# Attention layer's weights and first input on GpSimd's queue, in the place of in_proj's weights; first stripe's edge stores on ScalarE's queue

## The chip, the cores and the metric

The kernel runs on one core of one Trainium2 chip. The metric is the time of one execution on the device in microseconds (us). Several executions are measured and their median is compared. Times inside an execution come from one profiled execution and count from the start of its span, which runs from its first to its last instruction.

The engines are PE (TensorE: matmuls; PEld is its loading of weights), DVE (VectorE), ACT (ScalarE), POOL (GpSimd) and SP (SyncE). Each takes its own instructions in order. Transfers (DMA) are issued by an engine's queue and carried by 16 DMA engines.

## The reference

Two layers, each with a group norm in front and a residual behind, on an image batch of 4 x 384 channels x 64 x 64:

```python
# layer 0: a state-space layer over the 4096 tokens of an image
x = x + _L0_conv_ref(_gn(x), ...)
# layer 1: attention of every pixel to the 7 x 7 pixels around it, 12 heads of 32 channels
x = x + _L1_conv_ref(_gn(x), ...)

def _L1_conv_ref(x, w_qkv, b_qkv, w_proj, b_proj, rel_bias):
    ...
    qkv = jnp.einsum('oc,bchw->bohw', w_qkv, x) + b_qkv[None, :, None, None]
    ...
    q, k, v = (qkv[:, 0] * scale, qkv[:, 1], qkv[:, 2])
    pad = ((0, 0), (0, 0), (0, 0), (p, p), (p, p))
    k_pad = jnp.pad(k, pad, mode='edge')
    v_pad = jnp.pad(v, pad, mode='edge')
    logits = jnp.stack([jnp.einsum('bnchw,bnchw->bnhw', q, k_pad[..., di:di + H, dj:dj + W]) for di in range(ws) for dj in range(ws)], axis=-1)
    logits = logits + rel_bias.reshape(nh, ws * ws)[None, :, None, None, :]
    attn = jax.nn.softmax(logits, axis=-1)
    ...
    out = jnp.einsum('oc,bchw->bohw', w_proj, out) + b_proj[None, :, None, None]
```

## The kernel before

**Two stages.** `layer0` goes through 4 images of 16 chunks of 256 tokens; each chunk passes the input projection (L409, weights `w_in`), a causal convolution, the scan over 16 states (L623 on DVE, L635 on POOL) and the output projection (L695, weights `w_out`). Its result goes to a DRAM tensor `x1` for each image (L710) and is read back by `layer1`. `layer1` goes through 4 images of 8 stripes of 8 pixel rows. A stripe is prepared by `projected`, a generator whose steps are worked in between the blocks of the stripe before; only the first stripe is prepared alone, before any block.

**The first stripe.** `projected` loads eleven rows of `x1` into `xr` (L860), normalises them on DVE into `xn` (L869), computes the keys (L882 on PE, copied by ACT at L887, with edges copied by POOL at L895 to L903), then the values, two pixel rows at a time (L915, copied to `v` by DVE at L922), and then the queries (L945, L950). Matmuls of the first stripe write to the four PSUM banks of the tag `lg`; `v` has three buffers, so the fourth copy waits until everything stored from the first is done.

**The values in DRAM.** Padded values go to a DRAM tensor `vd` of 70 x 70 pixels. Each pixel row is written by three stores: the 64 pixels (L932, 96 KB), three copies of the first pixel (L933) and three of the last (L937, 4.5 KB each). The top row of the image goes to four rows of `vd`. For the first stripe these are 14 rows and so 42 stores. `window` (L963) then reads, for each block of 8 x 16 pixels, the 14 x 22 pixels around it into `vw`, by 14 loads.

**Weights.** At the head of `layer1`, `bias`, `w_qkv` and `w_pj` are allocated in the pool `wt`, in this order, which starts where the first pool of `layer0`, `w0`, started with `w_in`. `w_in` takes 18,432 bytes of each partition, `bias` 14,784, `w_qkv` 13,824 and `w_pj` 4,608. The mask and position terms `bias` are loaded from a DRAM tensor `bm` that was built during `layer0` (L1092). Nine small matmuls (L841, PSUM tile `pvb`) turn the bias of the values into one of the output, added to `pjb` by DVE (L846); `pjb` is first read at the end of a stripe (L1067). The group statistics of the last image (`group_stats`, L229; PE, DVE and one ACT step, `grs`) are computed after the first stripe is prepared, ahead of the first block.

**Order.** In both layers PE, DVE, ACT and POOL work in the order of the program text (`manual_schedule`). SP's transfers are ordered by a planner, which may put a transfer ahead of others written before it; SP takes the planned order one by one, and a transfer whose waits are not met holds up those behind it. Every transfer from SP or ACT counts up one of eight completion counters, taken in turn in the planned order, and first waits until the previous transfer on that counter has landed. In the kernel before all transfers are issued by SP.

Of the kernel before, what the change touches and what calls it, by code (L numbers as in the profile page):

```python
# [8 lines left out]
F32 = mybir.dt.float32  # L9
AF = mybir.ActivationFunctionType  # L10
ALU = mybir.AluOpType
# [3 lines left out]
P = 128  # L15
C = 384
NJ = C // P
# [31 lines left out]
def two_layers(  # L49
# [21 lines left out]
    nc = tc.nc  # L71
# [97 lines left out]
    with nc.allow_non_contiguous_dma(reason="small vectors, one element per partition"):  # L169
# [5 lines left out]
        qkb = column(qkv_b, 3 * NJ, "qkb", const)  # L175
        pjb = column(proj_b, NJ, "pjb", const)
# [15 lines left out]
    with tc.tile_pool(name="ps_fold", bufs=1, space=PSUM) as fps:  # L192
        pb0 = fps.tile([P, 512], F32, name="pb0")
        for m in range(2 * ND):
            for j in range(NJ):
                nc.tensor.matmul(
                    pb0[:, m : m + 1], w_in[:, j, m * P : (m + 1) * P], lnb[:, j : j + 1],
                    start=(j == 0), stop=(j == NJ - 1),
# [622 lines left out]
    def layer1(x1s, mvs, gms):  # L821
        scale = HD**-0.5
        with ExitStack() as es:
            es.enter_context(tc.manual_schedule(engines=in_step))
            ps_l = es.enter_context(tc.tile_pool(name="ps_l", bufs=4, space=PSUM))
            ps_t = es.enter_context(tc.tile_pool(name="ps_t", bufs=2, space=PSUM))
            ps_v = es.enter_context(tc.tile_pool(name="ps_v", bufs=1, space=PSUM))
            ps = es.enter_context(tc.tile_pool(name="ps1_", bufs=1, space=PSUM))
            wt = es.enter_context(tc.tile_pool(name="wt", bufs=1))
            w2 = es.enter_context(tc.tile_pool(name="v2_", bufs=2))  # L830

            bias = wt.tile([P, NH, NK], F32, name="bias")
            w_qkv = wt.tile([P, NJ, 3 * C], F32, name="w_qkv")
            nc.sync.dma_start(w_qkv, qkv_wT.rearrange("(k p) m -> p k m", p=P))
            w_pj = wt.tile([P, NJ, C], F32, name="w_pj")
            nc.sync.dma_start(w_pj, proj_wT.rearrange("(k p) m -> p k m", p=P))

            pvb = ps_t.tile([P, 512], F32, tag="pt", name="pvb")
            for m in range(NJ):
                for j in range(NJ):  # L840
                    nc.tensor.matmul(  # L841
                        pvb[:, m : m + 1], w_pj[:, j, m * P : (m + 1) * P],
                        qkb[:, 2 * NJ + j : 2 * NJ + j + 1],
                        start=(j == 0), stop=(j == NJ - 1),
                    )
            nc.vector.tensor_tensor(pjb, pjb, pvb[:, :NJ], ALU.add)  # L846
            vds = [dram.tile([WP, WP, C], F32, tag="vd", name=f"vd_{b}") for b in range(NB)]

            def bank(pool, tag):
                return pool.tile([P, 512], F32, tag=tag, name=f"{tag}_ps")  # L850

            def projected(b, s, h, pool=ps, tag="mm"):


                gm, vd = gms[b], vds[b]
                lo, hi = RB * s, min(HW, RB * s + RB + PAD)
                n = hi - lo
                xr = w2.tile([P, NJ, RB + PAD, HW], F32, tag="xr", name=f"xr_{b}_{s}")
                xn = w2.tile([P, NJ, RB + PAD, HW], F32, tag="xn", name=f"xn1_{b}_{s}", bufs=1)
                nc.sync.dma_start(  # L860
                    xr[:, :, :n, :].rearrange("p k r c -> p k (r c)"),
                    x1s[b][:, lo * HW : hi * HW].rearrange("(k p) t -> p k t", p=P),
                )
                q = w2.tile([P, NJ, NBLK, RB, CB], F32, tag="q", name=f"q_{b}_{s}")
                k = w2.tile([P, NJ, RW, WP], F32, tag="k", name=f"k_{b}_{s}")
                h["q"], h["k"] = q, k
                yield
                for j in range(NJ):
                    nc.vector.tensor_scalar(  # L869
                        xn[:, j, :n, :], xr[:, j, :n, :], gm[:, j, 0:1], gm[:, j, 1:2],  # L870
                        ALU.subtract, ALU.mult,
                    )

                old = 0 if s == 0 else PAD
                if s:
                    nc.sync.dma_start(k[:, :, : RW - RB, :], h["before"][:, :, RB:, :])
                for m in range(NJ):
                    for r0, r1 in ((0, PAD), (PAD, n)) if s == 0 else ((PAD, n),):
                        cols = (r1 - r0) * HW
                        pk = bank(pool, tag)  # L880
                        for j in range(NJ):
                            nc.tensor.matmul(  # L882
                                pk[:, :cols], w_qkv[:, j, C + m * P : C + (m + 1) * P],
                                xn[:, j, r0:r1, :].rearrange("p r c -> p (r c)"),
                                start=(j == 0), stop=(j == NJ - 1),
                            )
                        act(  # L887
                            k[:, m, PAD + r0 : PAD + r1, PAD : PAD + HW],
                            pk[:, :cols].rearrange("p (r c) -> p r c", c=HW),
                            AF.Identity, bias=qkb[:, NJ + m : NJ + m + 1],  # L890
                        )
                    yield
                new = k[:, :, PAD + old : PAD + n, :]
                edge = [P, NJ, n - old, PAD]
                nc.gpsimd.tensor_copy(  # L895
                    new[:, :, :, 0:PAD], new[:, :, :, PAD : PAD + 1].broadcast_to(edge)
                )
                nc.gpsimd.tensor_copy(
                    new[:, :, :, PAD + HW :],
                    new[:, :, :, PAD + HW - 1 : PAD + HW].broadcast_to(edge),  # L900
                )
                if s == 0:
                    nc.gpsimd.tensor_copy(  # L903
                        k[:, :, :PAD, :], k[:, :, PAD : PAD + 1, :].broadcast_to([P, NJ, PAD, WP])
                    )
                if s == NXT - 1:
                    nc.gpsimd.tensor_copy(
                        k[:, :, PAD + n :, :],
                        k[:, :, PAD + n - 1 : PAD + n, :].broadcast_to([P, NJ, RW - PAD - n, WP]),
                    )  # L910
                for r0 in range(old, n, 2):
                    rows = min(2, n - r0)
                    pv = bank(pool, tag)
                    for j in range(NJ):
                        nc.tensor.matmul(  # L915
                            pv[: rows * HW, :C],
                            xn[:, j, r0 : r0 + rows, :].rearrange("p r c -> p (r c)"),
                            w_qkv[:, j, 2 * C :],
                            start=(j == 0), stop=(j == NJ - 1),
                        )  # L920
                    v = w2.tile([P, C], F32, tag="v", name=f"v_{b}_{s}_{r0}", bufs=3)
                    nc.vector.tensor_copy(v[: rows * HW, :], pv[: rows * HW, :C])  # L922
                    for r in range(rows):
                        img = lo + r0 + r
                        src = v[r * HW : (r + 1) * HW, :]
                        to = [img + PAD]
                        if img == 0:
                            to = list(range(PAD + 1))
                        if img == HW - 1:
                            to = list(range(PAD + img, WP))  # L930
                        for y in to:
                            nc.sync.dma_start(vd[y, PAD : PAD + HW, :], src)  # L932
                            nc.sync.dma_start(  # L933
                                vd[y, 0:PAD, :].unsqueeze(0),
                                src[0:1, :].unsqueeze(1).broadcast_to([1, PAD, C]),
                            )
                            nc.sync.dma_start(  # L937
                                vd[y, PAD + HW :, :].unsqueeze(0),
                                src[HW - 1 : HW, :].unsqueeze(1).broadcast_to([1, PAD, C]),
                            )  # L940
                    yield
                for m in range(NJ):
                    pq = bank(pool, tag)
                    for j in range(NJ):
                        nc.tensor.matmul(  # L945
                            pq, w_qkv[:, j, m * P : (m + 1) * P],
                            xn[:, j, :RB, :].rearrange("p r c -> p (r c)"),
                            start=(j == 0), stop=(j == NJ - 1),
                        )
                    nc.vector.tensor_scalar(  # L950
                        q[:, m, :, :, :].rearrange("p b r c -> p r b c"),
                        pq.rearrange("p (r b c) -> p r b c", r=RB, b=NBLK),
                        qkb[:, m : m + 1], scale, ALU.add, ALU.mult,
                    )
                    yield
# [131 lines left out]

            todo = [(b, s) for b in range(NB) for s in range(NXT)]
            stripes = [{} for _ in todo]
            ahead = projected(*todo[0], stripes[0], ps_l, "lg")  # L1090
            next(ahead)
            nc.sync.dma_start(bias.rearrange("p h k -> p (h k)"), bm)  # L1092
            for _ in ahead:
                pass
            vw = window(*todo[0], 0)
            for part in group_stats(mvs[NB - 1], gms[NB - 1], ps, f"b{NB - 1}"):
                part()

# [124 lines left out]
```

## Time and profile before

| what | us |
|---|---|
| median of 4 runs | 8267.8 |
| lowest and highest | 8261.52 and 8272.43 |
| the profiled execution | 8261.52 |
| its span | 8259.5 |
| last matmul of layer 0 (L695) ends, about | 5931.4 |
| first matmul on the first stripe (L882) | 5946.5 |
| first matmul of the first block (L978) | 5987.45 |
| PE busy in the span | 7510.5 |
| DVE, POOL, ACT busy in the span | 6988.1, 6985.4, 5892.2 |
| mean granted TensorE clock (1 is full speed) | 0.949 |

The span is cut by the profile into forty slices. In the first 28, layer 0, PE, DVE, POOL and ACT are all busy for some eight tenths or more; in the last twelve, layer 1, PE is busy for nine tenths or more and the others for less. The DMA engines are busy for one to three tenths in nearly every slice. The passage between the layers is a small part of one slice, so it is read from the chain of waits, the timeline and windows of a few microseconds.

### The profile page before, as it was taken

The numbers are of one execution on the slowest core, as the hardware profiler recorded it, in microseconds if no ns is written. First come the engines' busy times: TensorE is split into PE (matmuls) and PEld (weight loads), VectorE is DVE, ScalarE is ACT, GpSimd is POOL, SyncE is SP. The second block draws the span as 40 slices with busy tenths as digits, with TensorE's granted clock in tenths as the row PEclk, the third lists the DMA queues.
The fourth block names the chain that finished last, engine by engine and source line by source line (L and its number), as shares of the span: only waits on it lengthen the run. The fifth ranks groups of instructions, "written<-read, shape, count | busy, mean of one in ns | idle before, by whom it ended". The sixth has DMA issues, their size and how long they took to land. (4 is left out here: it accounts for less than half of the span.)

```text
span 8259.5 us, 144369 instructions
## 1 busy us (share of the span) xinstructions
PE 7510.5 (91%) x48570; PEld 5814.9 (70%) x48570; DVE 6988.1 (85%) x12725; ACT 5892.2 (71%) x15613; POOL 6985.4 (85%) x4247
## 2 busy tenths in 40 slices
PE   7998998899899889988998999899799999999999
PEld 6777777777777777777777777777555555555555
DVE  5999999999999999999999999999666666666666
ACT  5888888888888888888878888888455455454455
POOL 4999999999999999999999999999677777677777
PEclk9999999999999999999999999999899999999999
DMA  3212211221121112112211211121223233232322
GB/s 109 65 60 70 74 58 57 69 68 59 65 76 62 55 63 75 59 65 72 66 53 59 69 58 55 62 69 51 81 84 87 85 88 88 81 88 84 89 82 64
DMA packets 327528, 583.40 MB, mean 71 GB/s; under 512 B 62940, under 2 KB 211180, under 8 KB 326660
## 3 DMA queue, kind: packets, MB, share of 16 engines
q1 hardware_dynamic: 326788, 574.17, 22.3%
q8 instruction: 387, 6.34, 0.3%
q14 instruction: 353, 2.89, 0.1%
HBM read 471.49 MB, written 84.73 MB: 67 GB/s over the span
## 5 line engine op out<-in xcount | busy, mean ns | idle before, releaser
L635 POOL TENSOR_TENSOR hs<-hs,C 128x1024 f32<-128x1024 f32 x1536 | 3617.8, 2364 | 459.8 <-ACT state L631 448.0
L623 DVE TENSOR_TENSOR_SCAN hs<-da,state,db 128x256 f32<-128x256 f32 x5760 | 3848.7, 729 | 121.5 <-issue 90.7
L96 ACT ACTIVATE da<-dt,nega 128x256 f32<-128x256 f32 x6144 | 2892.1, 475 | 885.4 <-DVE hs L623 840.1
L648 PE MATMUL y<-ident,hs 128*128 128x128 f32 x12288 | 1730.0, 293 | 586.5 <-POOL hs L635 355.1
L999 POOL TENSOR_SCALAR sg<-sg,rsum 128x308 f32<-128x308 f32 x1536 | 1620.8, 1076 | 639.7 <-DVE rsum L997 628.6
L648 PEld LDWEIGHTS y<-ident,hs 128*128 128x128 f32 x12288 | 1516.3, 151 | 882.1 <-POOL hs L635 518.4
L600 POOL TENSOR_TENSOR db<-dtx,B 128x1024 f32<-128x1024 f32 x640 | 1515.3, 2368 | 5.1
L409 PE MATMUL mm_ps<-xn,w_in 128*128 128x256 f32 x4608 | 1112.9, 388 | 1.9 <-DVE xn L380 1.9
L600 DVE TENSOR_TENSOR db<-dtx_ps,B 128x1024 f32<-128x1024 f32 x896 | 1064.8, 1200 | 0.7 <-ACT dtx_ps L593 0.7
L96 ACT ACTIVATE sg<-sg,mx 128x308 f32<-128x308 f32 x1536 | 828.7, 541 | 250.3 <-DVE mx L984 222.2
L984 DVE CUSTOM_DVE_ANT_0 sg<-lg_ps,bias 128x308 f32<-128x308 f32 x1536 | 643.1, 475 | 381.1 <-PE lg_ps L978 381.1
L409 PEld LDWEIGHTS mm_ps<-xn,w_in 128*128 128x128 f32 x4608 | 878.2, 196 | 113.4 <-DVE xn L380 2.6
L416 PE MATMUL mm_ps<-xb,dcv 128*128 128x256 f32 x3072 | 716.0, 379 | 0.0
L1027 ACT COPY tb<-pt_ps 88x512 f32<-88x512 f32 x384 | 222.2, 579 | 625.2 <-PE pt_ps L1023 625.1
L416 PEld LDWEIGHTS mm_ps<-xb,dcv 128*128 128x128 f32 x3072 | 572.2, 190 | 75.9 <-issue 0.3
L695 PE MATMUL mm_ps<-yg,w_out 128*128 128x256 f32 x2304 | 556.2, 383 | 0.0
L1014 DVE COPY ta<-pt_ps 110x512 f32<-110x512 f32 x768 | 492.4, 683 | 23.3 <-PE pt_ps L1009 23.3
L695 PEld LDWEIGHTS mm_ps<-yg,w_out 128*128 128x128 f32 x2304 | 438.7, 193 | 58.9
L1009 PE MATMUL pt_ps<-ident,sg 128*110 128x128 f32 x3072 | 417.6, 279 | 0.8 <-POOL sg L999 0.8
L1009 PEld LDWEIGHTS pt_ps<-ident,sg 128*110 128x110 f32 x3072 | 322.7, 133 | 77.9 <-issue 48.8
L882 PE MATMUL mm_ps<-xn,w_qkv 128*128 128x512 f32 (+2 forms) x612 | 278.0, 592 | 60.5 <-DVE xn L869 53.3
L978 PE MATMUL lg_ps<-k,q 32*128 32x308 f32 x3072 | 311.2, 473 | 0.0
(149 smaller groups left out, 10031.4 us busy)
## 6 DMA issues: line engine op xcount, KB each, us to landing
B<-bcrows SPq DMA_DIRECT2D x256, 512.0 KB
C<-bcrows SPq DMA_DIRECT2D x256, 512.0 KB
vw<-vd SPq DMA_DIRECT2D x1792, 33.0 KB
xr<-x SPq DMA_DIRECT2D x28, 1056.0 KB
vd<-v SPq DMA_DIRECT2D x280, 96.0 KB
xi<-in_x_dram SPq DMA_DIRECT2D x64, 384.0 KB
xo<-in_x_dram SPq DMA_DIRECT2D x64, 384.0 KB
x<-xo SPq DMA_DIRECT2D x64, 384.0 KB
```

The costliest lines, as they stand in the source:

```text
L96: ins = nc.scalar.activation(o, i, func, **kw)
L409: nc.tensor.matmul(pb[:, k, :], w_in[:, j, m * P : (m + 1) * P], xn[:, j, :], start=(j == 0), stop=(j == NJ - 1),)
L416: nc.tensor.matmul(pb[:, k, :], dcv[:, d, c, :], xb[:, d, c : c + T], start=(c == 0), stop=(c == KC - 1),)
L600: eng.tensor_tensor(db, dtx.unsqueeze(1).broadcast_to([P, NG, T]), h["B"][g], ALU.mult)
L623: nc.vector.tensor_tensor_scan(hs[:, j, :], da[:, k, :], dbs[I, m][:, j, :], state[:, d, n : n + 1] if I % NCHUNK else 0.0, ALU.mult, ALU.add,
L635: nc.gpsimd.tensor_tensor(hs, hs, h["C"][m % (NS // NG)], ALU.mult)
L648: nc.tensor.matmul(y[:, d % 2, half, :], hs[:, k, half * P : (half + 1) * P], ident, is_transpose=True, start=(first and half == 0 and d % ...
L695: nc.tensor.matmul(po, w_out[:, d, m * P : (m + 1) * P], h["yg"][d // 2][:, d % 2, :], start=False, stop=(d == ND - 1),)
L984: nc.vector.tensor_tensor_reduce(sg[:, hh, :], lg[:, :NK], bias[:, 4 * m + hh, :], -1.0, BIG, ALU.add, ALU.min, mx[:, hh : hh + 1],)
L999: nc.gpsimd.tensor_scalar(sg[:, hh, :], sg[:, hh, :], rs[:, hh : hh + 1], None, ALU.mult)
L1009: nc.tensor.transpose(pt[: KN[c], col : col + P], sg[:, 2 * pair + hh, KOFF[c] : KOFF[c] + KN[c]], ident,)
L1014: nc.vector.tensor_copy(t[: KN[0], :, :].rearrange("p a q -> p (a q)"), pt[: KN[0], :])
```

## The change

The two loads of the weights and the first load of `xr` move from SP's queue to POOL's. `bias` is allocated after `w_qkv` and `w_pj`. The nine matmuls and the addition for the bias of the values become a function that is called after the first stripe is prepared and its first window load is written. The edge stores of the first stripe move from SP's queue to ACT's; those of all other stripes stay on SP. The load of `bias`, all other loads and the stores of the 64 pixels stay on SP.

```diff
+            w_qkv = wt.tile([P, NJ, 3 * C], F32, name="w_qkv")
+            nc.gpsimd.dma_start(w_qkv, qkv_wT.rearrange("(k p) m -> p k m", p=P))
+            w_pj = wt.tile([P, NJ, C], F32, name="w_pj")
+            nc.gpsimd.dma_start(w_pj, proj_wT.rearrange("(k p) m -> p k m", p=P))
             bias = wt.tile([P, NH, NK], F32, name="bias")
-            w_qkv = wt.tile([P, NJ, 3 * C], F32, name="w_qkv")
-            nc.sync.dma_start(w_qkv, qkv_wT.rearrange("(k p) m -> p k m", p=P))
-            w_pj = wt.tile([P, NJ, C], F32, name="w_pj")
-            nc.sync.dma_start(w_pj, proj_wT.rearrange("(k p) m -> p k m", p=P))
-
-            pvb = ps_t.tile([P, 512], F32, tag="pt", name="pvb")
-            for m in range(NJ):
-                for j in range(NJ):
-                    nc.tensor.matmul(
-                        pvb[:, m : m + 1], w_pj[:, j, m * P : (m + 1) * P],
-                        qkb[:, 2 * NJ + j : 2 * NJ + j + 1],
-                        start=(j == 0), stop=(j == NJ - 1),
-                    )
-            nc.vector.tensor_tensor(pjb, pjb, pvb[:, :NJ], ALU.add)
+
+            def values_bias():
+
+                pvb = ps_t.tile([P, 512], F32, tag="pt", name="pvb")
+                for m in range(NJ):
+                    for j in range(NJ):
+                        nc.tensor.matmul(
+                            pvb[:, m : m + 1], w_pj[:, j, m * P : (m + 1) * P],
+                            qkb[:, 2 * NJ + j : 2 * NJ + j + 1],
+                            start=(j == 0), stop=(j == NJ - 1),
+                        )
+                nc.vector.tensor_tensor(pjb, pjb, pvb[:, :NJ], ALU.add)
+
...
-            def projected(b, s, h, pool=ps, tag="mm"):
+            def projected(b, s, h, pool=ps, tag="mm", first=False):
...
-                nc.sync.dma_start(
+                (nc.gpsimd if first else nc.sync).dma_start(
                     xr[:, :, :n, :].rearrange("p k r c -> p k (r c)"),
                     x1s[b][:, lo * HW : hi * HW].rearrange("(k p) t -> p k t", p=P),
                 )
...
                             nc.sync.dma_start(vd[y, PAD : PAD + HW, :], src)
-                            nc.sync.dma_start(
+                            edge_dma = (nc.scalar if first else nc.sync).dma_start
+                            edge_dma(
                                 vd[y, 0:PAD, :].unsqueeze(0),
                                 src[0:1, :].unsqueeze(1).broadcast_to([1, PAD, C]),
                             )
-                            nc.sync.dma_start(
+                            edge_dma(
                                 vd[y, PAD + HW :, :].unsqueeze(0),
                                 src[HW - 1 : HW, :].unsqueeze(1).broadcast_to([1, PAD, C]),
                             )
...
-            ahead = projected(*todo[0], stripes[0], ps_l, "lg")
+            ahead = projected(*todo[0], stripes[0], ps_l, "lg", first=True)
             next(ahead)
             nc.sync.dma_start(bias.rearrange("p h k -> p (h k)"), bm)
             for _ in ahead:
                 pass
             vw = window(*todo[0], 0)
+            values_bias()
             for part in group_stats(mvs[NB - 1], gms[NB - 1], ps, f"b{NB - 1}"):
                 part()
```

## The prediction

> **What bounds the kernel now.** I read the page first: PE is busy in 91% of the span and holds the largest share of the chain that ended last, 25%, and no DMA line of that chain reaches 1%. So a change to queues can only matter where PE stands still. The diff touches one such place, the passage from the state-space layer to the attention layer, so I read the chain of waits there (start, length, engine, tile, line; times from the span's start):
>
> ```profile
> 5928.81 2.60 PE mm_ps L695 x12
> 5931.96 7.73 DMA x<-xo
> 5939.77 5.95 DMA xr<-x
> 5945.81 0.66 DVE xn L869
> 5946.50 13.08 PE lg_ps L882 x36
> ...
> 5979.00 1.77 DMA vd<-v
> 5981.15 0.55 DVE v L922
> 5981.70 1.98 DVE q L950 x3
> ```
>
> Two links are not compute: the last x1 store and, behind it, the first xr load (5931.96 to 5945.72), and later a wait for stores to vd. Everything after this passage follows PE's queue, so what it gains or loses reaches the end. Next the timeline of the same stretch:
>
> ```profile
> 5931.48 0.37 SPq L834 DMA_DIRECT2D w_qkv<-in_qkv_wT_dram  x1
> 5931.96 0.42 SPq L710 DMA_DIRECT2D x<-xo  x1
> 5932.43 0.48 SPq L836 DMA_DIRECT2D w_pj<-in_proj_wT_dram  x1
> 5939.77 0.37 SPq L860 DMA_DIRECT2D xr<-x  x1
> 5940.19 0.48 SPq L1092 DMA_DIRECT2D bias<-bm  x1
> 5941.31 3.97 PE L841 MATMUL pvb<-qkb,w_pj 128*128 128x1 f32 x18 [9.91 <-DMA w_pj<-in_proj_wT_dram]
> 5973.01 0.56 DVE L922 COPY v<-lg_ps 128x384 f32<-128x384 f32 x1 [7.02 <-DMA vd<-v]
> 5976.83 0.56 DVE L922 COPY v<-lg_ps 128x384 f32<-128x384 f32 x1 [3.26 <-PE lg_ps L945]
> 5981.15 0.55 DVE L922 COPY v<-lg_ps 64x384 f32<-64x384 f32 x1 [3.76 <-DMA vd<-v]
> ```
>
> The weights start only at 5931.48, with the last out_proj matmul. pvb's 3.97 us lie wholly in PE's wait for xr. The last three of six v copies wait until their buffer's earlier stores have landed (the one put down to PE too: the last store of its buffer was issued 1.98 us before it). Last, the windows (busy time of PE, PEld, DVE, ACT, POOL, then granted clock, DMA share, GB/s):
>
> ```profile
> 5934.00:5936.00 2.00, 0.00 (x0) 0.00 (x0) 0.00 (x0) 0.00 (x0) 0.00 (x0) 0.50 1.03 412
> 5936.00:5938.00 2.00, 0.00 (x0) 0.00 (x0) 0.00 (x0) 0.00 (x0) 0.00 (x0) 0.50 0.98 365
> 5938.00:5940.00 2.00, 0.00 (x0) 0.00 (x0) 0.00 (x0) 0.00 (x0) 0.00 (x0) 0.50 1.07 392
> ```
>
> While x1's store is awaited, the DMA engines are full, 390 GB/s in the mean; and PE's clock stands at 0.50.
>
> **Part A, the loads.** In the built program of the changed kernel w_qkv and w_pj do lie exactly where w_in lay, but the wait in front of the w_qkv load is still for the last L695 matmul and the last decay of ScalarE (the pool is released as one). So GpSimd issues it at about 5931.5, as SyncE did; the 155 us since in_proj's last matmul (5776.7) are not used. What changes is what is in flight ahead of xr. SyncE now issues bias (1.892 MB) at 5931.5, and x1's store (0.393 MB) stands behind it in the place it had behind w_qkv. GpSimd adds w_qkv (1.769) and w_pj (0.590); then its xr load waits for x1's landing, as before.
>
> Check on the old stretch: x1 landed at 5939.69 with 2.162 MB through; at 390 GB/s that is 5.54 us, so the stream began at 5934.15. New: 4.645 MB are ahead of xr, 11.9 us, done at 5946.05. x1 lands at 5940.0 at the earliest (SyncE's 2.286 MB alone) and 5946.05 at the latest; with equal shares for the two queues it would be 5945.9. I take 5945, since GpSimd should start a little later. Then xr: before, 5.95 us from issue to landing, with nothing ahead. Now SyncE issues o, xr of stripe 1, o, o (1.87 MB) at that moment. With equal shares xr's 1.081 MB take 5.5 us, plus 2.4 us from issue to a full stream (5931.48 to 5934, rounded, in the old stretch): 7.9.
>
> The trace has no GpSimd DMA. Its issue is bounded by SyncE's 0.37 us and by GpSimd's longest row, 2.36 us (L635); nearest is GpSimd's one-input 128x630 copy, 0.71 us (L903), which I add in full. xr lands at 5945 + 7.9 + 0.7 = 5953.6 against 5945.72: **+7.9 us**. Low end: all bytes ahead and xr at the best rate of the stretch, 430 GB/s: 5.726 MB, 13.3 us, 5947.5: +1.7. High end: x1 at 5946.05, xr behind all of 2.95 MB (7.6 us) plus 2.4 and 2.36: 5958.4, +12.7. GpSimd has nothing to do until the k edges (5960.44 before), so its waiting holds up nobody.
>
> The Trainium skill (DMA: Bandwidth & Descriptors, "Issuing engines are not separate DMA queues") speaks against this part: transfers from all engines share the same 16 DMA engines, and another issuer saves only issuing time. The rows of 0.98 to 1.07 DMA share agree; by that rule alone the edge stores would still gain what rival 3 works out, and the sum would be about +3 instead of +15. The same page ("Anatomy of one DMA — SWDGE (gpsimd) path") gives a GpSimd transfer about 2.0 us plus bytes over 436 GB/s, an estimate of 4.5 us for xr alone; with that in place of the 8.6 above the sum would be about +11; no run here shows it yet.
>
> **Part B, the first stripe.** Let t0 be the end of the first v copy (5962.13). Before, SyncE issued 42 stores to vd, three per row, 0.49 + 0.62 + 0.62 us: third-last, second-last and last v copies at t0+10.9, +14.7 and +19.0, the statistics' ScalarE step (grs) at 5986.03, t0+23.9. Now 14 stay and 28 go to ScalarE. Each transfer counts up one of eight completion counters and first waits for that counter's previous transfer; a store takes 2.0 us from issue to the one who waits (5971.03 to 5973.01). In the built program the first ten edge stores alternate between only two counters: five pairs of 2.0 us, the tenth issued at +8.7, landed at +10.7. So the fourth copy is not earlier. The planner also put 23 window loads (0.43 us each with gaps: 42 took 17.69 us) in SyncE's queue right after its first nine stores. From the twelfth on, ScalarE's edge stores sit on counters that those loads use: the twelfth waits for the 18th load (issued +12.8, landed +14.9), the thirteenth until +16.2, the fourteenth until +17.1. The fourteenth lands at +19.1; only then is the second v buffer free: the fifth copy comes at +19.15 instead of +14.7. Carried on, the sixth comes at +23.2, and ScalarE issues its last edge store at +29.7, free at +30.3. Behind these 28 on ScalarE wait grs and the first exponentials.
>
> PE's last query group needs the PSUM bank of the fifth copy: it starts at +19.75 after some 5 us without work. The clock fell within 2.4 us of the last matmul at 5931.4 and within 4.4 us at 5980.6, so I take it at half speed, where the six passes of L882 at 5991.66 took 4.61 us: end +24.35. Now pvb follows, its cover gone: 3.97 us at half clock (about 2.0 if full), +28.3. Then psm and gmean 0.6, and from gmean to grs 2.43 us as before (5983.60 to 5986.03): +31.3 against +23.9, **+7.4 us**. With a full clock ScalarE's +30.3 binds: +6.5. With a round trip of 2.3 us, or 1.0 us for an issue on ScalarE, it is free at 32 to 34: +10. The copy pjb, now behind the queries, is 0.16 us and inside this. After grs the chain runs as before. GpSimd and the other queues have no new work, and the next stripes' order on SyncE differs only in some xr, o and out transfers, whose waits are met.
>
> Sum 7.9 + 7.4 = 15.3 on a profiled time of 8261.52 (span 8259.5 and 2.0 around it); that execution is 6.3 below the median of four, 8267.8, to which I add: **8283 us**.
>
> **Rivals.** (1) GpSimd builds transfers slowly. If its 384 rows cost three times its 2.36 us, each takes 7.1: w_qkv to 5938.6, w_pj to 5945.7, xr to 5952.8, landed 5.5 + 2.4 later at 5960.7: +15 with +7.4 is 8290. For it: every GpSimd row is slow per element; against: all but the last hide behind x1's store. (2) The placing works after all: the weights go out when GpSimd's last product ends (5918.2) and are in before 5931. Then x1 lands at 5940, xr about where it was; +7.4 or a little less is left: 8275. Against it stands the wait in the built program. (3) Not slower: edge stores run free on ScalarE, because counters come back faster than I count. Ten at 0.62 us and a 2.0 us landing free the first buffer at +8.2, the next at +10.7, and the chain to grs ends near +19.2: -4.7. With the low half of part A (+2.9) that is 8266. It decides from the point where the twelfth edge store goes out before about t0+8; for it SyncE's stores, issued back to back on eight counters, against it the two alternating ones.
>
> **How the numbers follow.** A measurement of this kernel tells about 0.2%, 16.5 us, from no change. The forecast case, +15 with its own range 8274 to 8292, gets 0.74: with the middle just below the mark, 0.36 above and 0.38 below it. Rival 1: 0.12, slower. Rival 2: 0.07, within. Rival 3: 0.07, 0.05 within and 0.02 faster. So 0.02 faster, 0.50 within, 0.48 slower. The range, 8272 to 8294, leaves out most of rival 3 and the far ends of rival 1 and of part A.
>
> **What would show it.** In the new profile: the GpSimd load of w_qkv starting at the last L695 matmul, not before; x1's store landing at about 13 us after its issue instead of 7.7; xn of stripe 0 some 8 us later from that matmul; the fifth v copy 19 us after the first one's end; ScalarE issuing edge stores for 30 us. I am wrong if xn starts within 2 us of its old distance, if the edge stores come every 0.65 us, or if a later stripe waits where it did not.

## The result, and the profile after

The changed kernel takes 8278.63 us (median of 41 runs, 8270.73 to 8287.59), the kernel before 8265.13 us on the same chip (61 runs, 8259.01 to 8276.3): a ratio of 1.0015, with a 95% interval of 1.0011 to 1.002. It is slower by 9 to 17 us. The prediction was 8283 us, 15.3 above before.

First the chain of waits of the changed kernel, in the passage between the layers (start, length, what, tile, line; the changed kernel has its lines a few numbers further down; in all chains shown, pieces of at most 0.5 us, most of them marked `issue`, are left out between the lines):

```profile
5935.51 2.60 PE mm_ps L695 x12
...
5938.14 0.37 ACT xo L708
...
5938.62 12.79 DMA x<-xo
...
5951.98 9.84 DMA xr<-x
...
5961.99 0.66 DVE xn L874
...
5978.72 2.82 DMA vd<-v
...
5994.67 2.01 DMA vw<-vd
5996.70 1.96 DMA vd<-v
...
5998.79 0.57 DVE v L927
...
5999.40 5.49 PE lg_ps L951 x6
6004.89 2.21 PE pvb L845 x18
...
6009.72 0.66 ACTq L943
6010.43 0.26 ACT grs_b L96
```

The two transfers at the head of the passage have grown from 7.73 and 5.95 us to 12.79 and 9.84. Further down the wait for `vd` is no longer one link of 1.77 us, but a series that runs by way of window loads (`vw<-vd`), which before had no part in it, and it ends with ScalarE's last edge store in front of the statistics' step `grs`. The timeline of the same stretch shows who issues what, and when:

```profile
5938.18 0.33 SPq L1098 DMA_DIRECT2D bias<-bm  x1
...
5938.62 0.37 SPq L710 DMA_DIRECT2D x<-xo  x1
5938.77 0.95 POOL L835 DMA_DIRECT2D w_qkv<-in_qkv_wT_dram  x1 [13.96 <-ACT xo L708]
...
5951.98 0.76 POOL L865 DMA_DIRECT2D xr<-x  x1 [11.48 <-DMA x<-xo]
...
5984.66 10.36 SPq L969 DMA_DIRECT2D vw<-vd  x23
...
5989.74 0.66 ACTq L939 DMA_DIRECT2D vd<-v  x1
...
5994.34 0.66 ACTq L943 DMA_DIRECT2D vd<-v  x1
...
5998.79 0.56 DVE L927 COPY v<-lg_ps 128x384 f32<-128x384 f32 x1 [7.53 <-DMA vw<-vd]
...
6009.72 0.66 ACTq L943 DMA_DIRECT2D vd<-v  x1
```

`w_qkv` goes out 0.63 us after the last copy to `xo` starts, not 155 us earlier. ScalarE has issued eleven of its edge stores by 5990.4; the twelfth waits until 5994.34, while SyncE issues 23 window loads, and the last goes out at 6009.72.

I measure the passage from the start of the last copy to `xo` (L708) to the first score matmul, and split it at the first normalisation `xn` and at t0, the end of the first v copy. All runs in one table; "medians" is the median minus that of the kernel before on the same chip (11 runs against 21 to 33; 41 against 61 in the first row of the changed kernel), the other columns come from each run's one profiled execution:

| run | medians | ratio (95%) | to xn | xn to t0 | t0 to score | passage |
|---|---|---|---|---|---|---|
| before | | | 14.4 | 16.3 | 25.3 | 56.0 |
| changed | +13.5 | 1.0015 (1.0011, 1.002) | 23.9 | 16.7 | 33.2 | 73.7 |
| a2_changed | +13.8 | 1.0019 (1.001, 1.0028) | 23.3 | 16.9 | 32.8 | 73.1 |
| e1_loads_only | +8.6 | 1.0011 (1.0002, 1.002) | 23.9 | 16.7 | 25.1 | 65.7 |
| e2_edges_only | +4.9 | 1.0006 (0.9997, 1.0015) | 14.4 | 16.3 | 33.3 | 63.9 |
| e3_bias_behind | +9.7 | 1.0012 (1.0003, 1.002) | 15.8 | 15.6 | 33.2 | 64.6 |
| e4_xr_on_sync | +11.4 | 1.0014 (1.0005, 1.0023) | 19.4 | 17.2 | 34.0 | 70.6 |
| e5_loads_after_edges | +3.6 | 1.0002 (0.9993, 1.0011) | 23.4 | 16.9 | 23.4 | 63.7 |
| e6_loads_by_need | -4.1 | 0.9993 (0.9984, 1.0002) | 10.1 | 16.8 | 25.0 | 51.9 |
| e7_stores_merged | -10.9 | 0.9988 (0.9979, 0.9996) | 9.9 | 18.3 | 21.7 | 49.9 |
| e8_all_on_sync | -11.0 | 0.9986 (0.9977, 0.9995) | 8.4 | 15.9 | 25.3 | 49.6 |
| e9_rows_apart | -15.6 | 0.9983 (0.9974, 0.9992) | 8.4 | 17.3 | 20.4 | 46.1 |

A time is known to about 7 us here, a passage to a few tenths (kernels that have a stage in common agree within 1.2 us in it, mostly within 0.6). So the experiments are judged by the passage first; the medians follow it in direction, with differences of up to 6 us.

### The profile page after: what moved, and what is told of

It reads as the page before. It is cut to its first block, busy times and chain, and to the rows that moved or that the text cites. A ratio compares the mean times of both kernels' runs of the same rounds, so it can differ in the third digit from the quotient of the medians.

```text
span 8279.0 us, 144377 instructions
## 1 busy us (share of the span) xinstructions
PE 7506.7 (91%) x48570; PEld 5813.3 (70%) x48570; DVE 6987.8 (84%) x12725; ACT 5892.3 (71%) x15613; POOL 6988.6 (84%) x4250
## 5 line engine op out<-in xcount | busy, mean ns | idle before, releaser
L695 PE MATMUL mm_ps<-yg,w_out 128*128 128x256 f32 x2304 | 554.5, 382 | 0.0
L1020 DVE COPY ta<-pt_ps 110x512 f32<-110x512 f32 x768 | 492.5, 683 | 23.3 <-PE pt_ps L1015 23.3
L695 PEld LDWEIGHTS mm_ps<-yg,w_out 128*128 128x128 f32 x2304 | 437.7, 192 | 58.6
```

Source lines behind the costliest of these rows:

```text
L695: nc.tensor.matmul(po, w_out[:, d, m * P : (m + 1) * P], h["yg"][d // 2][:, d % 2, :], start=False, stop=(d == ND - 1),)
L1020: nc.vector.tensor_copy(t[: KN[0], :, :].rearrange("p a q -> p (a q)"), pt[: KN[0], :])
```

## The experiments

**The changed kernel again.** In its first profile the passage is 17.7 us longer than before's, but the rest of layer 1 is 4.9 shorter. Is that part of the change?

> The changed kernel once more, as it is. In its first profile the passage from the last L695 matmul to the first score matmul is 17.7 us longer than in before's, while the rest of layer 1 behind it is 4.9 us shorter (2267.1 against 2272.0). Theory that the 4.9 are a matter of that one execution: here the passage is 17 to 18.5 us longer again and the rest is 2271 to 2275, as in four other kernels with the same code behind the passage (2272.5, 2274.5, 2273.1, 2274.2). Rival, the delay of the passage is systematically made up later: the rest is 2266 to 2269 again.

Measured: passage 17.1 us longer, rest 2272.4 us, as before's 2272.0. The 4.9 us belonged to that one execution. The rest varies between 2267 and 2275 us over all kernels, and event by event the differences come in steps of about 1.7 us, up and down, where the code is the same. The granted clock accounts for them: the traces' clock records switch between full and half in stretches that are whole multiples of 3.41 us (in before's passage half clock for 17.07, full for 34.13, half for 10.24), and half clock through one such stretch loses 1.7 us of full clock. From the first score matmul to the end, half clock adds up to 31.4 us in the changed kernel's first profile, 43.2 in before's and 43.5 in this one's; with half of that taken off, the rest is 2251.4, 2250.5 and 2250.7 us, and 2249.8 to 2251.8 over all twelve profiles.

**Part A alone: the loads.**

```diff
-                            edge_dma = (nc.scalar if first else nc.sync).dma_start
+                            edge_dma = nc.sync.dma_start
```

> The changed kernel with the edge stores of the first stripe back on SyncE: part A of the sum, and the bias of the values behind the first stripe, stay. My theory (the sum of the two parts): the first normalisation xn starts about 9.5 us later after the last L695 matmul than in the kernel before (23.9 instead of 14.4), the v copies keep the old rhythm (third-last, second-last and last at t0+10.9, +14.7, +19.0), grs comes at about t0+25 (the old +23.9 and one or two for the eighteen small matmul passes, now uncovered), and the time is 9 to 11 us above before, 2 to 4 below the changed kernel. Rival, the loads cost nothing in the end because their delay is made up later in layer 1 (the changed kernel's trace has 4.9 us less than before's between the first score matmul and the end): then the time is within 5 us of before. Rival, the two parts are not additive (a late start of the stripe makes the edge stores expensive): grs after t0+28.

Measured: xn at 23.9, then t0 to score 25.1 us as before, and +8.6 us in the medians. Part A is +9.6 us of passage, and the delay is not made up later. The expected one or two microseconds for `pvb` are not there. Its timeline (the copies and the passes of `pvb`):

```profile
5997.27 2.06 PE L845 MATMUL pvb<-qkb,w_pj 128*128 128x1 f32 x18
...
5997.96 0.55 DVE L927 COPY v<-lg_ps 64x384 f32<-64x384 f32 x1 [3.42 <-DMA vd<-v]
...
6000.47 0.14 DVE L264 COPY gmean_b<-psm_b 32x1 f32<-32x1 f32 x1
```

PE runs `pvb` while DVE still waits for `vd` with the sixth copy, behind which the statistics' `gmean` stands on DVE anyway: a new cover in place of the one that was lost.

**Part B alone: the edge stores.**

```diff
-                            nc.sync.dma_start(
+                            edge_dma = (nc.scalar if first else nc.sync).dma_start
+                            edge_dma(
```

> The kernel before with one thing changed: the edge stores of the first stripe go to ScalarE's queue. My theory: the loads are as before (xn 14.4 us after the last L695 matmul), the first ten edge stores go out in pairs every 2.0 us since they alternate between two completion counters, the fifth v copy is at t0+18 to 20 and the sixth at t0+22 to 24 instead of +14.7 and +19.0, ScalarE issues edge stores until about t0+30, and grs is at t0+29 to 31 instead of +23.9: the time is 5 to 8 us above before. Rival, the edge stores are slow in the changed kernel only because GpSimd's loads and SyncE's late ones are still in flight beside them: then edge stores here come every 0.65 us, grs is at or ahead of t0+24, and the time is that of before or some 4 us less.

Measured: to xn 14.4 as before, t0 to score 33.3 instead of 25.3. The timeline has the same pattern without any load on GpSimd:

```profile
5971.73 10.81 SPq L964 DMA_DIRECT2D vw<-vd  x23
...
5976.82 0.66 ACTq L934 DMA_DIRECT2D vd<-v  x1
...
5982.02 0.66 ACTq L938 DMA_DIRECT2D vd<-v  x1
...
5986.09 0.56 DVE L922 COPY v<-lg_ps 128x384 f32<-128x384 f32 x1 [7.45 <-DMA vd<-v]
```

The eleventh edge store is at 5976.82, the twelfth 5.2 us later, the fifth copy ends at t0+20.9 and the sixth at +25.4, 0.9 and 1.4 us past the ends of the ranges expected. The rival (slow only beside GpSimd's loads) falls. The two parts are additive: 9.6 + 7.9 = 17.5 against 17.1 and 17.7 for both. In the medians this run, taken by itself (0.9997 to 1.0015), can't be told from before. `pvb` stays in its old place here, so PE's part is done early (`psv` ends at 5995.27); `grs` still comes at t0+31.8, behind ScalarE's last edge store (5997.52). So at the end of part B it is ScalarE's issuing, and not PE, that holds `grs`.

**The counters.** The same 28 stores on ScalarE, but the planner is told to put the first stripe's window loads behind the last edge store, without any wait:

```diff
-                        nc.sync.dma_start(
+                        ins = nc.sync.dma_start(
                             vw[rr * CW : (rr + 1) * CW, c, :],
...
+                        if (b, s) == (0, 0):
+                            tc.add_manual_dep(
+                                ins.ins,
+                                last_edge[0],
...
+                                reason="window loads behind the edge stores",
```

> The changed kernel, with the window loads of the first stripe put behind the last of its edge stores in the planned order; nothing else changes, the 28 edge stores stay on ScalarE. The loads on SyncE then no longer take up the completion counters that the edge stores wait for. My theory (part B: shared counters hold up ScalarE's stores): the fourth, fifth and sixth v copies end about t0+10, +13 and +16 instead of +12.0, +20.1 and +24.4, the last edge store is issued at about t0+21 instead of +31.0, the first score matmul comes at t0+22 to 26 instead of +33.2, and the time is 7 to 11 us below the changed kernel. Rival, ScalarE's stores are slow by themselves (its issue, or transfers of 4.5 KB from two queues at once): then pairs every 2 us and more go on, the last edge store comes at t0+27 or later, the first score matmul at t0+29 or later, and the time is within 4 us of the changed kernel.

Its chain of waits:

```profile
5981.97 0.66 ACTq L945
5982.67 0.67 ACTq L941
5983.38 0.66 ACTq L945
5984.08 0.66 ACTq L941
...
5991.90 1.98 DMA vd<-v
5994.16 0.55 DVE v L929
```

From the fourth on, the stores go out every 0.70 us; the last three copies end at t0+10.7, +13.7 and +16.7 (expected +10, +13, +16; in the changed kernel they start at +12.0, +20.1 and +24.4 and end 0.6 later), t0 to score is 23.4 instead of 32.8 (a2), and the medians are 10.3 us below the changed kernel on the same chip. So the stall of part B is neither ScalarE's issuing nor the small transfers: it is the completion counters shared with loads that the planner put early. The semaphore records of the changed kernel's trace agree: its twelfth, thirteenth and fourteenth edge stores go out at t0+15.7, +16.9 and +18.0, each 0.02 us after the 18th, 21st and 23rd window load has landed. With free counters ScalarE's queue even gains 1.7 us against SyncE's (25.1 in e1).

**Bias out of x1's way.**

```diff
-            nc.sync.dma_start(bias.rearrange("p h k -> p (h k)"), bm)
+            nc.gpsimd.dma_start(bias.rearrange("p h k -> p (h k)"), bm)
```

> The changed kernel with the load of the mask and position terms (bias, 1.892 MB) moved from SyncE's queue to GpSimd's, where it stands behind xr; SyncE then issues x1's store first. Theory of the bytes ahead (the prediction's): x1's store shares the engines with w_qkv alone and lands some 6 to 7 us after its issue instead of 12.8, xr has w_qkv, w_pj, x1 and some of the o loads ahead of it, some 4.9 MB with itself, 12.6 us at 390 GB/s and 2.5 to start, so xn starts 15 to 17 us after the last L695 matmul instead of 23.9, and the time is 7 to 9 us below the changed kernel. Rival, GpSimd's queue is slow by itself: xr needs 9.8 us or more from its issue wherever that is, w_qkv takes 11.9 us or more although bias is gone, x1's landing still gains, and xn starts 17 to 20 us after that matmul. Rival, x1's landing is late for another reason than the bytes (it waits for something of GpSimd's): x1 still lands 12 to 13 us after its issue and the time is that of the changed kernel.

Its chain of waits:

```profile
5935.78 2.55 DMA x<-xo
...
5938.98 12.00 DMA xr<-x
5951.16 0.66 DVE xn L874
```

x1's store takes 2.55 us instead of 12.79, far less than the 6 to 7 expected: with no `bias` ahead of it on its own queue its packets are through at 5937.96, before `w_qkv`'s first at 5938.17. In the changed kernel `bias` kept its first packet back for 6.4 us, until 5945.01, and by then `w_qkv` was under way beside it. `xr` now waits behind `w_qkv` and `w_pj` on GpSimd's and takes 12.00. xn comes at 15.8, inside the 15 to 17 that the bytes gave, though x1's part of that sum was wrong. `w_qkv` lands 9.0 us after its issue, not 11.9, so the rival's fixed slowness falls. The passage gains 8.5 to 9.1 us on the two profiles of the changed kernel; the medians, 4 us closer to before than the changed kernel's in two different comparisons, can't confirm that size.

**xr back on SyncE.**

```diff
-                (nc.gpsimd if first else nc.sync).dma_start(
+                nc.sync.dma_start(
```

> The changed kernel with the first load of xr back on SyncE's queue, ahead of the o loads and of the second stripe's xr; the weights stay on GpSimd and bias ahead of x1's store. x1's store should land 12 to 13 us after its issue as in the changed kernel. Theory that xr's 9.8 us are GpSimd's own queue and issue, and its place beside 1.87 MB of SyncE's: xr then takes 6 to 7 us from issue to landing (5.95 before), xn starts 3 to 4 us earlier than in the changed kernel, and the time is 3 to 4 us below it. Rival, the 9.8 us are bytes that are in flight ahead of xr anyway: xr takes 9 us or more here too and the time is that of the changed kernel.

```profile
5937.77 12.95 DMA x<-xo
5950.87 5.66 DMA xr<-x
5956.66 0.66 DVE xn L874
```

In its chain x1's store takes 12.95 us again, but `xr` 5.66 instead of 9.84. xn starts 4.5 us earlier than in the changed kernel (3 to 4 expected), and the medians are some 2 us lower, within their uncertainty. The run changes two things at once: who issues `xr`, and whether the loads of `o` and of the second `xr` stand behind it in its queue or beside it in another. The traces' records of single packets say where most of the 4.2 us goes, 3.7 of them until the first packet (worked out from each transfer's issue and the first packet on its queue):

| transfer | issued by | first packet after |
|---|---|---|
| bias, `o` (changed); xr (e4); x1 (e3) | SyncE | 0.96, 0.97; 1.03; 0.88 us |
| w_qkv, xr (changed) | GpSimd | 4.5, 4.7 us |
| w_qkv (e4); first part of w_qkv (e6) | GpSimd | 4.4; 5.3 us |
| w_qkv (e3, with only x1's 0.39 MB on SyncE ahead of it) | GpSimd | 2.15 us |

**Loads ordered by need.** `xr` in a pool of its own, inside the space that `w_in`'s pool had, so that it no longer waits for x1's store; first on SyncE; weights in three parts on GpSimd.

```diff
+            xp = es.enter_context(tc.tile_pool(name="xp", bufs=2))
...
+            for part in (1, 2, 0):
+                cols = slice(part * C, (part + 1) * C)
+                nc.gpsimd.dma_start(
...
-                xr = w2.tile([P, NJ, RB + PAD, HW], F32, tag="xr", name=f"xr_{b}_{s}")
+                xr = xp.tile([P, NJ, RB + PAD, HW], F32, tag="xr", name=f"xr_{b}_{s}")
```

> Kernel before with the loads ordered by when they are needed: xr gets a pool of its own that lies wholly in the space of w_in's pool, so that its first load waits for the last L695 matmul but not for x1's store to land, and stands first on SyncE's queue, x1's store behind it; GpSimd loads w_qkv in three parts (keys, values, queries), then w_pj, then bias; the bias of the values is computed behind the first stripe; all edge stores stay on SyncE. Theory (bytes ahead, and the wait for x1's landing, set the start): xr shares the engines with the first weights only, some 2.2 to 2.5 MB at 390 GB/s and 2.5 us to start, so xn starts 8 to 9.5 us after the last copy to xo starts instead of 14.4 (before) and 23.9 (changed), the first score matmul follows t0 by 25 us as before, and the time is 4 to 7 us below before. Rival, a GpSimd transfer is slow by itself (11.9, 12.6 and 9.8 us from issue to landing in the changed kernel's trace): the keys' weights land 9 us or more after their issue although only some 1.7 MB are ahead of or beside them, PE's first key matmul waits for them, and the time is within 3 us of before.

Its timeline:

```profile
5940.68 0.36 SPq L871 DMA_DIRECT2D xr<-x  x1
...
5941.27 2.50 POOL L838 DMA_DIRECT2D w_qkv<-in_qkv_wT_dram  x3 [13.96 <-ACT xo L708]
...
5950.72 1.76 DVE L880 TENSOR_SCALAR xn<-xr,gm_b 128x704 f32<-128x704 f32 x3 [7.87 <-DMA x<-xo]
```

xn at 10.1, a little later than the 8 to 9.5 of my theory, and the line says why: xn's wait ends with x1's store (`<-DMA x<-xo`), not with `xr`. By the packet records `xr`'s bytes were in at 5946.5, 5.8 us after its issue, while those of x1's store, which stands behind `xr` and then shares the engines with GpSimd's queue, ran until 5949.97. `xr` has left the space that waits for that store, but `xn` still lies in it. The passage is 4.1 us shorter than before's, and the medians say the same (-4.1), though the interval reaches 1.0002. The rival is not excluded: the keys' weights needed 8.5 us to land, until 5949.8, and would have held the first key matmul nearly as long.

**The same, all on SyncE.** The keys' part first, then x1's store, `xr`, the other parts, `w_pj`, `bias`.

```diff
-                nc.gpsimd.dma_start(
+                nc.sync.dma_start(
                     w_qkv[:, :, cols], qkv_wT[:, cols].rearrange("(k p) m -> p k m", p=P)
...
+            weights(1)
...
             next(ahead)
+            weights(2)
+            weights(0)
```

> The run with the loads by need, with all its loads on SyncE's queue and none on GpSimd's: the keys' part of w_qkv first, then x1's store, xr, the values' part, the queries' part, w_pj, bias. In the run before it the first part of w_qkv landed 8.5 us after GpSimd issued it and xr 9.9 us after SyncE did. Theory (a GpSimd transfer moves its first bytes some 4 to 5 us after its issue, SyncE's after some 2): 2.06 MB are through when xr lands, 5.3 us at 390 GB/s and 2.5 to start, so xn starts 7.5 to 8.8 us after the last copy to xo starts instead of 10.1, the first score matmul follows t0 by 25 us, and the time is 1 to 3 us below that run. Rival, only bytes count and not the issuer: the order by need is the same to within half a megabyte, xn starts 10 to 11 us after that copy, and the time is the same.

```profile
5931.68 0.38 ACT xo L708
5932.21 0.42 SPq L710
5932.68 7.26 DMA xr<-x
5940.07 0.66 DVE xn L880
```

In its chain xn waits for `xr` again, which lands 7.26 us after its issue with 2.06 MB through; xn comes at 8.4, inside the 7.5 to 8.8 expected, and the medians are 11 us below before. But the run doesn't tell my theory from another: x1's store has moved ahead of `xr` as well (its bytes were in at 5936.90, 4.7 us after its issue), and it was that store that held xn in e6. What the issuer costs rests on e4 and on the table of first packets (which has 0.9 to 1.0 us for SyncE, not the 2 of my theory).

**Fewer stores, statistics in between.** A pair of rows is stored by three transfers instead of six; the statistics' steps go between the steps of the first stripe.

```diff
+                            store(vd[y : y + 2, PAD : PAD + HW, :], v)
+                            for to, at in ends_:
+                                store(
+                                    vd[y : y + 2, to : to + PAD, :],
...
+            for _ in ahead:
+                if stats:
+                    stats.pop(0)()
```

> As the run with the loads by need, and in the first stripe a pair of rows is stored by three transfers instead of six (the 64 pixels of both rows, the first and the last pixels of both), 27 stores instead of 42, and the steps of the last group statistics are put between the steps of the first stripe. Theory (the issue of stores and the empty statistics chain set t0 to the first score matmul): the last store is issued at about t0+16, the fifth and sixth v copies end at about t0+11 and +13, PE is dense until the queries and the eighteen small passes are done, the first score matmul comes at t0+18 to 21 instead of +25.3, and the time is 4 to 7 us below the run with the loads by need, some 10 to 13 below before. Rival, something else holds the first scores (the key edges of GpSimd or the load of bias, which now stands last on GpSimd's queue): the first score matmul or its DVE step waits for those, at t0+24 or later, and nothing is gained over the run with the loads by need.

Measured: t0 to score 21.7, the fifth and sixth copies at +16.6 and +20.9, later than the +11 and +13 expected and than before. The score comes earlier all the same, probably because of the statistics: `grs` is now at t0+1.7 and no longer behind the copies. The run doesn't separate the two changes. Three windows of two microseconds, in the columns of the prediction's windows:

```profile
5974.00:5976.00 2.00, 2.00 (x6) 0.80 (x6) 0.00 (x0) 0.00 (x0) 0.00 (x0) 1.00 0.13 50
5976.00:5978.00 2.00, 1.34 (x4) 0.47 (x3) 0.63 (x2) 0.00 (x0) 0.00 (x0) 1.00 0.13 49
5978.00:5980.00 2.00, 2.00 (x6) 0.85 (x5) 0.00 (x0) 0.00 (x0) 0.00 (x0) 1.00 0.13 50
```

A DMA share of 0.13 is two of sixteen engines, window after window. So I gave each row its own transfer of 64 pixels again:

```diff
-                            store(vd[y : y + 2, PAD : PAD + HW, :], v)
+                            for r in range(2):
+                                store(vd[y + r, PAD : PAD + HW, :], v[r * HW : (r + 1) * HW, :])
```

> The run with merged stores, with the loads all on SyncE's queue as in the run beside it, and the 64 pixels of each row stored by a transfer of their own again (2 x 64 x 384 becomes twice 64 x 384; the first and last pixels of two rows stay merged), 32 stores. In the run with merged stores the stretch in which the 2 x 64 x 384 stores are under way has 2.1 packets in flight in the mean and 50 GB/s, and the fourth to sixth v copies waited for them, at t0+10.7, +16.6 and +20.9. Theory (a transfer whose outer dimension is two is spread over two of the sixteen DMA engines only): here the last three copies end at t0+9 to 11, +12 to 14 and +14 to 16, the first score matmul comes at t0+18 to 20.5 instead of +21.7, and the time is 3 to 6 us below the run with merged stores. Rival, the merged edge stores of two rows are the slow ones, or three merged stores in a row wait for each other: the copies stay at +16 and +20 and the gain is that of the loads alone, 1 to 3 us.

Its chain of waits:

```profile
5937.76 7.28 DMA xr<-x
...
5945.92 5.50 PE lg_ps L893 x12
...
5959.75 4.07 PE lg_ps L926 x12
...
5968.92 4.21 PE lg_ps L926 x12
5973.13 7.92 PE lg_ps L986 x18
5981.05 1.90 PE pvb L851 x18
5982.96 0.77 PE lg_ps L1019 x8
```

The copies end at t0+10.2, +12.4 and +14.8, and from the first key matmul to the first score the chain holds PE alone; no wait is left in it. Against e7 the first score comes 1.3 us earlier after t0, though the copies gain 4 and 6: PE's own work is what is left. The passage is 46.1 us against before's 56.0, the time 15.6 us below before (ratio 0.9974 to 0.9992), and lower than both kernels of this case.

## Why the prediction came out as it did

**Placing the weights early does nothing.** Right. GpSimd issues `w_qkv` at 5938.77, behind the last L695 matmul (5938.11) and the last copy to `xo` (5938.51).

**x1's landing at 13 us.** The size is right: 12.79. The reason was bytes ahead, and e3 and the packets show which: `bias`, in the same queue, and then `w_qkv` beside it. "Equal shares" was not how it went, though. The packet records show `bias` alone at 384 to 399 GB/s from 5941 until `w_qkv`'s first packet at 5943.28, and from 5945 x1's packets of 1 KB and `w_qkv`'s of 4.6 KB taken in equal numbers (72 and 71 in 5946 to 5947), which gives x1 some 75 GB/s and `w_qkv` 330. The two errors cancel, so that 12.79 came so close to 13 is luck.

**xr in 8.6 us.** Mis-sized: 9.84, plus 0.57 instead of 0.08 us between x1's landing and the issue. The term was 2.4 + 0.7 to start and 5.5 for the bytes; measured are 4.7 to the first packet and 5.1 from there to the landing. So part A is +9.5 instead of +7.9, inside its bounds. The Trainium skill's rule for a GpSimd transfer (DMA: Bandwidth & Descriptors, "Anatomy of one DMA — SWDGE (gpsimd) path": 2.0 us plus bytes over 436 GB/s) gives an estimate of 4.5 us for `xr` from end to end. The trace has 9.84, of which the time to the first packet alone, with SyncE's transfers under way, is 4.7; here the measurement decides.

**The counters, pairs of 2.0 us, the fifth copy at +19.15.** Right, and shown by e2, e5 and the semaphore records. The steps were some 1 us short: twelfth store +15.7 instead of +14.9, fifth copy starting at +20.1, sixth +24.4 instead of +23.2, last edge store +31.0 instead of +29.7. The 23 loads began at t0+6.0 and came 0.45 us apart where I had counted 0.43 from before's 42; the 18th, for which the twelfth store waits, went out at +14.0 instead of +12.8 and landed 1.6 us later instead of 2.1.

**The last query group at half clock, then pvb.** The group at half clock and `pvb` behind it did occur, with sizes off in opposite directions: the six passes took 5.49 us (4.61 predicted) and `pvb` 2.21 (3.97 predicted). By the trace's clock records the granted clock was 0.50 from 5998.56 to 6005.39, through all six passes, and 1.00 for the 3.4 us behind that, most of `pvb`. grs came at t0+31.7 (predicted +31.3). But this was not the path that bound: ScalarE's own issuing ends at 6010.38, half a microsecond behind PE's chain (psv ends at 6009.82), and 1.3 us behind it in a2. The prediction had the two at +30.3 and +31.3 and took the other one. So its term for `pvb` was worth nothing: e2, where `pvb` is done long before, has the same t0 to score (33.3). Part B is +7.8 against +7.4, and that closeness is in part luck: ScalarE's end was set too early by 1.4 us, and the path chosen in its place was 1 us longer.

**The sum.** 9.5 + 0.4 (xn to t0, the clock came back a little later) + 7.8 = 17.7 in the passage against the 15.3 predicted. The medians say 13.5 and 13.8. The gap is not settled: the profiled execution's shorter rest, less time at half clock, belongs to one profile only, and a2 shows no such thing. In nine of the eleven rows below before's, the medians lie 1 to 6 us under the difference of the passage, so the gap is not peculiar to this kernel. The time predicted was 8283 against 8278.6; of the 4.4, 2.7 are the median of before (8267.8 from four runs, 8265.1 from 61).

**Rivals.** GpSimd building transfers slowly was half right: an issue costs 0.76 to 0.95 us, far from the 7.1 that this rival assumed, but the bytes start late. Early placing and free edge stores didn't occur; e5 shows what the latter would have been worth once the loads are out of the way, t0 to score 23.4. The Trainium skill's rule that issuing engines are not separate DMA queues (DMA: Bandwidth & Descriptors, "Issuing engines are not separate DMA queues") holds in these traces for the rate: 404 to 417 GB/s in the windows from 5946 to 5950 with two issuers, 365 to 412 with one before. For the start of a transfer it made a difference who issued it (the table of first packets).

## What to carry to other kernels

Before a transfer is moved to another queue, list what then stands ahead of the transfers that the next stage waits for, in each queue, and which completion counters the moved ones share with whatever a planner has put early. A queue that is "free" is worth little where the wait in front of it is a memory release or a counter; here the order by need on one queue (e8, 11.0 us below before), and one tile taken out of the space that is released late, were worth more than two further issuers.

## What the runs showed of the hardware that was not expected

- The first packet of a GpSimd transfer with nothing ahead of it in its own queue came 2.15 us after its issue beside little traffic (e3), 4.1 to 5.3 us with more of SyncE's transfers under way (4.1 for `xr` in e1, 5.3 in e6); a SyncE transfer's after 0.9 to 1.0 us. Whether GpSimd's own work or the engines' order makes the difference was not tried.
- Two queues were served packet by packet: 72 to 75 packets a microsecond each from 5946 to 5950 in the changed kernel, so packets of 1 KB got some 75 GB/s beside 330 for packets of 4.6 KB.
- A store of 2 x 64 x 384 elements held a DMA share of 0.13 and 50 GB/s, as if spread over two engines; with 64 x 384 twice (e9) the copies that wait for it came 4 to 6 us earlier. The Trainium skill (DMA: Bandwidth & Descriptors, "Why a DMA increments its semaphore by 16 and not by 1") says that a transfer runs on the largest number of engines, sixteen at most, that divides the slowest dimension of both its sides; the 0.13, two of sixteen, agrees with it.
- The granted clock changed in whole multiples of 3.41 us, and executions of the same code differed in steps of about 1.7 us (the rest of layer 1 took 2267 to 2275 us).
